# Border of a graph layer and the next hop: two subtractions moved behind VectorE's last additions, and a product's accumulators paired otherwise

## The chip, the cores and the metric

The kernel runs on one core of one Trainium2 chip. Times are microseconds of device time for one execution; lower is better. Several executions give a median; one more execution, on the same kernel, was recorded by the hardware profiler, and all views of the profile come from that one.

## What is computed

Two graph layers on features `x` of 8 batches, 2048 nodes and 64 channels, with one row-normalised adjacency matrix `adj` of 2048 x 2048. Each layer ends in a residual and a layernorm. Cut to what matters:

```python
# layer 0: I, A, 2AA-I applied to x, then a 64x64 weight of each node's own (16 parts), bias
w = einsum('nd,dkio->nkio', embedding, weight)          # d = 16, k = 3
x_g = einsum('knm,bmc->bnkc', A_stack, x)
x = layernorm(x + einsum('bnki,nkio->bno', x_g, w) + b)
# layer 1: x, Ax, 2AAx-x (twice, with the same A), one shared weight
x = layernorm(x + x_cat @ weight + bias)
```

Every row of `adj` holds one value at its nonzero places, so the kernel splits it into a 0/1 pattern and a factor per row, and multiplies with the pattern. The features go into the matmuls as two parts, a high half (rounded to fp32r) and a low half (the rest), one matmul for each.

## The kernel before

The program has five stretches: two hops (products of the pattern with the features) for layer 0; the node mixing of layer 0, node tile by node tile (16 tiles of 128 nodes); a third hop and a fourth for layer 1; and the final layernorm. The change lies at the border between the mixing of the last tile (t = 15) and the third hop.

**Order.** Each engine carries out its instructions in the order in which the program writes them (`ordered`), so the order is written out by hand. In the mixing loop, `at[n]` lists the side work that is written ahead of piece n of a tile, and `at[8]` what is written after the last piece.

**Mixing of a tile** (`mix0`, L402). Eight pieces, each a product in PSUM (L409), which is then weighted and added up. Pieces of four channels' worth (`by_four`, L425) are added into `acc` by VectorE, four instructions each (L433). Pieces by batch go over ScalarE into `aside` (L423), which GpSimd sums (L440, three instructions) and adds to `acc` (L445). For the last tile the pieces are (0,0), (0,1), (0,4), (1,0), (0,5), (1,1), (1,4), (1,5); the last two are VectorE's. Then comes the projection of the tile before (`project`, L458: matmuls L466, six ScalarE copies L475), and the layernorm of this tile (L362 to L380), whose result is transposed on TensorE (L300) inside the third hop, at the steps (0,5) and (0,6) of it (`last_transposed`, `last_projected`).

**The third hop** (`seven_products`, L586, called at L833). A product of 2 x 2 blocks in seven products, each with 8 contraction steps, 56 steps in all. Each step has 8 matmuls (L664): for each of two halves of the output (i), first the high half and then the low half of the features, each over two column blocks. A product accumulates in two PSUM buffers, `sums[p % 2]`, one for i = 0 and one for i = 1, so products alternate between two pairs of buffers. The high halves are made by ScalarE (`high`, L234), the low halves by VectorE (`low`, L238: features minus high half), the pattern operand by a ScalarE cast (L652). For the first four steps these are written early (`early`, L842), within the last tile's mixing:

```python
            at[6] += [(("add",), 0), lambda: got.update(hT=transpose(h, "hT")), lambda: early(2, "y_high")]
            at[7] += [(("sum",), 1), lambda: early(2, "y_low"), lambda: early(3, "y_high")]
            at[8] += [(("add",), 1), lambda: early(3, "y_low")]
```

**PSUM.** One pool of four buffers, two banks each (`bank`, L84), serves all of it: pieces, transposes, projections and the hop's sums. A new tile takes a buffer when it is first written, and its first matmul waits for the last reader of what was there. The four sums of the hop are named at the first step (L659):

```python
                if p == 0 and kk == 0:
                    sums.extend([bank("accT") for _ in range(2)] for _ in range(2))
                acc, hl, S = sums[p % 2], got["hl"], got["s"]
```

Of the kernel before, what the change touches and what calls it, by code (L numbers as in the profile page):

```python
# [39 lines left out]
def pattern(  # L40
# [43 lines left out]
    def bank(name):  # L84

        return psum.tile([P, 2, 512], F32, tag="ps", name=name)
# [146 lines left out]
    def high(src, to):  # L233
        ordered(nc.scalar.copy(to[0], src))  # L234
# [348 lines left out]
        (S4, "B22", (0, 1)), ((0, 1), "B21", (0, 0)), ((1, 1), "T4", (1, 0)),  # L583
    )

    def seven_products(s, to, sums, more, wait=4, raw=()):  # L586

        kept = {}

        def sum_of_y(kk, name):


            def quarter(half, b):
                return z[s][kk + KK * (half - 1)][:, (b - 1) * BC : b * BC]

            def add(to, a, b, op):
                ordered(nc.vector.tensor_tensor(to, a, b, op))  # L600
                return to

            if name[0] == "B":
                return quarter(int(name[1]), int(name[2]))
            if name == "T2":
                if kk % 2 == 0:
                    tag = "acc" if kk < KK // 2 else "ln_sq"
                    kept[kk // 2] = work.tile([P, 2, BC], F32, tag=tag, name="t2")
                y = kept[kk // 2][:, kk % 2]
                return add(y, add(y, quarter(2, 2), quarter(1, 2), ALU.subtract), quarter(1, 1), ALU.add)  # L610
            if name == "T4":
                y = kept[kk // 2][:, kk % 2]
                return add(y, y, quarter(2, 1), ALU.subtract)
            y = xcpool.tile([P, BC], F32, tag="ln_xc", name="y")
            a, b = (quarter(1, 2), quarter(1, 1)) if name == "T1" else (quarter(2, 2), quarter(1, 2))
            return add(y, a, b, ALU.subtract)

        def step(p, kk):
            which, name, finished = PRODUCTS[p]

            def sum_y(got):
                got["y"] = sum_of_y(kk, name)

            def y_high(got):
                hl = hpool.tile([P, 2, BC], F32R, tag="hl", name="hl")
                got["hl"] = [hl[:, 0], hl[:, 1]]
                if name == "T4":
                    got["y"] = kept[kk // 2][:, kk % 2]
                elif name[0] == "B":
                    sum_y(got)  # L630
                high(got["y"], got["hl"])

            def y_low(got):
                low(got["y"], got["hl"])

            def load_sum(got):
                if which in raw:
                    return
                got["raw"] = rawp.tile([P, 2, Q], BF16, tag="raw", name="raw")
                if which == (0, 0):  # L640
                    load(nc.sync, got["raw"], corner[kk])
                elif isinstance(which, tuple):
                    load(nc.sync, got["raw"], quarters[kk, :, which[0]])
                else:
                    load(nc.sync, got["raw"], sums_of[kk, :, :, which, :].rearrange("g m n -> m g n"))

            def operands(got):
                if which in raw:
                    got["s"] = places(slab(kk, 0, HALF))
                else:  # L650
                    s = spool.tile([P, 2, Q], F32R, tag="s", name="s")
                    ordered(nc.scalar.copy(s, got["raw"]))  # L652
                    got["s"] = s.rearrange("p g n -> p (g n)")
                if loads:
                    load(nc.sync, *loads.pop(0))

            def use(got):
                if p == 0 and kk == 0:
                    sums.extend([bank("accT") for _ in range(2)] for _ in range(2))  # L659
                acc, hl, S = sums[p % 2], got["hl"], got["s"]  # L660
                for i in range(2):
                    for h in range(2):
                        for c in range(2):
                            nc.tensor.matmul(  # L664
                                acc[i][:, c], lhsT=hl[h][:, i * P : (i + 1) * P], rhs=S[:, c * 512 : (c + 1) * 512],
                                start=(kk == 0 and h == 0), stop=(kk == KK - 1 and h == 1),
                            )
                if p == 3:
                    sum_of_y(kk, "T4")
                for f in more.get((p, kk), ()):  # L670
                    f()
                if kk < KK - 1:
                    return
                if p < 6:
                    todo.extend([nothing] * wait)
                for i in range(2):
                    for c in range(2):
                        todo.append(lambda i=i, c=c: put(acc[i][:, c], i, c))
                while p == 6 and todo:
                    todo.pop(0)()  # L680
                todo.extend(more.get(p, ()))

            def put(src, i, c):

                src = src.rearrange("p (t n) -> p t n", n=P)

                def add(where, first, op=ALU.add):
                    ordered(nc.vector.tensor_tensor(to(*where, i, c), to(*first, i, c), src, op))  # L688

                product = PRODUCTS[p]  # L690
                if product is M1:
                    ordered(nc.scalar.copy(to(0, 0, i, c), src))
                elif product is M6:
                    add((0, 1), (0, 0))
                elif product is M7:
                    add((1, 0), (0, 1))
                elif product is M5:
                    add((1, 1), (1, 0))
                    add((0, 1), (0, 1))
                else:  # L700
                    add(finished, finished, ALU.subtract if product is M4 else ALU.add)

            before = [(5, sum_y)] if name in ("T1", "T2", "T3") else []
            return before + [(4, y_high), (3, y_low), (4, load_sum), (3 if which in raw else 2, operands), (0, use)]

        return [step(p, kk) for p in range(7) for kk in range(KK)]
# [116 lines left out]
    def quarter_back(a, b, which):  # L823
# [11 lines left out]
        (0, 6): [last_projected],  # L835
        **{(2 + t // KK, t % KK): [lambda t=t: add_bias(t)] for t in range(NT)},
        3: quarter_back(1, 1, 1), 4: quarter_back(0, 1, 0), 5: quarter_back(0, 0, 1),
    }, wait=2)

    third_got = {}  # L840

# [11 lines left out]
    s = ("load_sum", "operands")  # L853
# [3 lines left out]
    for t in range(NT):  # L857
        got, last = {}, t == NT - 1
        at = [[] for _ in range(9)]
        n1, n2, n3 = [lambda: next(norm)] * 3 if t else [nothing] * 3  # L860

        if not last:
            following, of_x, of_hop, of_second = coming
            of_hop = of_hop()
            at[1] += [go(of_x)] * (1 if t else 3)
            at[2] += [go(of_hop), n1, go(of_hop), go(of_hop), n2]
            if t + 2 < NT:
                at[2] += [lambda: times_r(t + 2)]
                at[4] += [lambda: got.update(coming=operands(t + 2))]
            at[3] += [n3, go(of_second), lambda: got.update(acc=begin_sum(t + 1))]  # L870
            at[4] += [go(of_second), go(of_second)]
            at[6] += [(("sum", "add"), 0)]
            at[7] += [lambda: got.update(hT=transpose(h, "hT"))] if t else []
            pieces = [(0, 0), (0, 4), (0, 5), (1, 2), (0, 1), (1, 3), (1, 4), (1, 5)]
        else:
            at[1] += [n1, n2]
            at[2] += [n3, lambda: early(0, "y_high", *s)]
            at[3] += [(("sum",), 0), lambda: early(0, "y_low")]
            at[4] += [lambda: early(1, "y_high", *s)]
            at[5] += [lambda: early(1, "y_low")]  # L880
            at[6] += [(("add",), 0), lambda: got.update(hT=transpose(h, "hT")), lambda: early(2, "y_high")]
            at[7] += [(("sum",), 1), lambda: early(2, "y_low"), lambda: early(3, "y_high")]
            at[8] += [(("add",), 1), lambda: early(3, "y_low")]
            pieces = [(0, 0), (0, 1), (0, 4), (1, 0), (0, 5), (1, 1), (1, 4), (1, 5)]
        norm_now = mix0(t, tt, acc, at, pieces)
        if t:
            project(t - 1, got["hT"])
        if "coming" in got:
            coming = got["coming"]
            next(coming[1])  # L890
            next(coming[1])
        norm = norm_now
        h = next(norm)
        if not last:
            tt, acc = following, got["acc"]
# [34 lines left out]
    sums = keep.tile([P, G, B], F32, tag="sums", name="sums")  # L930
# [445 lines left out]
```

## Time and profile before

| what | value |
|---|---|
| median of three executions | 764.98 us (764.36 to 765.15) |
| the profiled execution | 764.04 us, of which the span is 762.3 us |
| TensorE matmuls, busy | 753.6 us, 99% of the span |
| VectorE, busy | 560.2 us, 73% |
| ScalarE, busy | 406.7 us, 53% |
| GpSimd, busy | 269.7 us, 35% |
| granted TensorE clock | 0.999 |
| third hop's and second hop's matmuls (L664) | 896, 390 ns each |

How to read it: the engines work side by side, so an engine's busy time says little unless it sets the end. The end of a matmul is modelled and overlaps with the next, so a recorded gap on TensorE is shorter than the time lost; starts are the surer measure. In a row of the timeline the first number is the start in us from the span's start, the second how long the row lasts, `x4` how many instructions are merged in it, and the brackets say how long the engine was idle ahead of it and for whom. In the list of waits, the numbers are the total, how often, and the longest.

### The profile page before, as it was taken

How to read it: one execution, taken by the hardware profiler on the slowest of the kernel's cores; microseconds unless marked ns; L12 is line 12 of the kernel's file. 1: busy time of each engine (PE TensorE's matmuls, PEld its weight loads, DVE VectorE, ACT ScalarE, POOL GpSimd, SP SyncE). 2: the span in 40 equal slices, each digit the busy share in tenths (PEclk: the TensorE clock that was granted, in tenths of full speed). 3: DMA queues.
4: the chain of work that ended last, by engine and by line, in shares of the span. 5: the costliest groups of instructions: out<-in, count | busy, mean ns of one | idle time of the engine just before them, and what ended most of it. 6: DMA issues, size and time to landing. Idle time of an engine off the chain costs nothing.

```text
span 762.3 us, 16926 instructions
## 1 busy us (share of the span) xinstructions
PE 753.6 (99%) x6634; PEld 660.6 (87%) x6634; DVE 560.2 (73%) x1159; ACT 406.7 (53%) x896; POOL 269.7 (35%) x297
## 2 busy tenths in 40 slices
PE   9999999999999999999999999999999999999996
PEld 6888888888889999999999999998888888888885
DVE  6768867678757888888888888877688648668663
ACT  5456533877745555555555555558887663112111
POOL 0000000000026877777777777777100000011441
PEclk9999999999999999999999999999999999999999
DMA  8998996555520000000000000003454444565631
GB/s 325 346 393 282 350 312 233 154 177 162 171 69 17 20 20 15 20 18 16 16 16 17 15 16 3 2 16 87 135 167 151 130 154 142 175 177 175 208 127 46
DMA packets 73558, 96.69 MB, mean 127 GB/s; under 512 B 4864, under 2 KB 48384, under 8 KB 73344
## 3 DMA queue, kind: packets, MB, share of 16 engines
q1 hardware_dynamic: 62064, 76.66, 31.8%
q10 hardware_dynamic: 11408, 18.89, 6.6%
q8 instruction: 54, 0.88, 0.5%
q14 instruction: 32, 0.26, 0.1%
HBM read 76.65 MB, written 18.87 MB: 125 GB/s over the span
## 4 chain that ended last, share of the span: by engine, by line
PE 98%; DVE 1%; issue 0%; ACT 0%; DVEq 0%
PE pm L409 36%; PE accT L664 27%; PE acc L254 15%; PE a L254 10%; PE accT L254 6%; PE pu L466 2%; PE pt L300 1%; PE first L143 1%; PE accT L814 1%; DVE acc L433 1%; PE accT L466 0%; PE accT L153 0%; PE accT L300 0%; ACT sq L994 0%; DVE z L289 0%
## 5 line engine op out<-in xcount | busy, mean ns | idle before, releaser
L433 DVE SCALAR_TENSOR_TENSOR acc<-pm,pack_sb,acc 128x256 f32<-128x256 f32 x376 | 181.0, 482 | 44.0 <-PE pm L409 32.0
L409 PE MATMUL pm<-wh,hl 64*128 64x512 f32 (+1 forms) x1332 | 208.0, 303 | 0.0
L664 PE MATMUL accT<-s,hl 128*128 128x512 f32 x896 | 205.9, 390 | 0.8 <-DVE acc L433 0.8
L409 PE MATMUL pm<-wm,parts 64*128 64x512 f32 (+1 forms) x1332 | 203.5, 296 | 0.0
L409 PE MATMUL pm<-wl,parts 64*128 64x512 f32 (+1 forms) x1332 | 203.4, 296 | 0.0
L664 PEld LDWEIGHTS accT<-s,hl 128*128 128x128 f32 x896 | 167.5, 188 | 36.5 <-issue 1.6
L409 PEld LDWEIGHTS pm<-wh,hl 64*128 64x128 f32 x1332 | 130.9, 187 | 4.0 <-issue 0.4
L409 PEld LDWEIGHTS pm<-wl,parts 64*128 64x128 f32 x1332 | 130.8, 187 | 3.7
L409 PEld LDWEIGHTS pm<-wm,parts 64*128 64x128 f32 x1332 | 130.5, 187 | 3.8
L652 ACT CAST s<-raw 128x1024 fp32r<-128x1024 bf16 x104 | 109.9, 1057 | 37.9 <-ACT hl L234 23.4
L254 PE MATMUL acc<-hl,s 128*128 128x512 f32 x512 | 116.8, 390 | 0.0
L254 PEld LDWEIGHTS acc<-hl,s 128*128 128x128 f32 x512 | 96.2, 188 | 20.5 <-issue 0.3
L423 ACT ACTIVATE aside<-pm,pack_sb 128x128 f32<-128x128 f32 x272 | 74.0, 383 | 48.9 <-PE pm L409 48.1
L715 POOL TENSOR_TENSOR z<-z,rrow 128x512 f32<-128x512 f32 x16 | 21.1, 1320 | 212.4 <-DVE z L688 212.4
L234 ACT CAST hl<-z 128x256 fp32r<-128x256 f32 (+1 forms) x96 | 47.7, 515 | 60.1 <-PE acc L254 24.1
L440 POOL TENSOR_TENSOR aside<-aside 128x1024 f32<-128x1024 f32 (+2 forms) x51 | 75.3, 1476 | 4.2 <-ACT aside L423 1.6
L254 PE MATMUL a<-hl,s 128*128 128x512 f32 (+1 forms) x352 | 73.4, 370 | 0.0
L254 PEld LDWEIGHTS a<-hl,s 128*128 128x128 f32 x352 | 61.9, 188 | 11.3
L320 POOL TENSOR_TENSOR parts<-parts 128x512 fp32r<-128x512 f32 x45 | 58.2, 1294 | 35.1 <-DVE parts L314 27.5
L238 DVE TENSOR_TENSOR hl<-z,hl 128x512 fp32r<-128x512 f32 (+1 forms) x96 | 54.7, 577 | 12.9 <-ACT hl L234 10.1
L287 POOL TENSOR_TENSOR z<-z,got 128x512 f32<-128x512 f32 x3 | 4.8, 1631 | 144.4 <-ACT got L286 144.4
L254 PE MATMUL accT<-hl,s 128*128 128x512 f32 x192 | 44.3, 390 | 0.0
(136 smaller groups left out, 814.4 us busy)
## 6 DMA issues: line engine op xcount, KB each, us to landing
raw<-in_adj SPq DMA_DIRECT2D x58, 512.0 KB, 6.1
raw<-sums_of SPq DMA_DIRECT2D x64, 256.0 KB, 2.9
sums_of<-z ACTq DMA_DIRECT2D x16, 512.0 KB, 6.6
raw<-quarters SPq DMA_DIRECT2D x32, 256.0 KB, 2.7
raw<-in_adj SPq DMA_DIRECT2D x16, 384.0 KB, 3.5
quarters<-seen ACTq DMA_DIRECT2D x16, 256.0 KB, 5.8
xt<-in_xT SPq DMA_DIRECT2D x16, 256.0 KB, 2.7
z<-in_x SPq DMA_DIRECT2D x15, 256.0 KB, 6.8
```

Of the source, the lines that this page charges most:

```text
L234: ordered(nc.scalar.copy(to[0], src))
L238: ordered(nc.vector.tensor_tensor(to[1], src, to[0], ALU.subtract))
L254: nc.tensor.matmul(accs[i], lhsT=s[:, i * P : (i + 1) * P], rhs=hl[h], start=(first and h == 0), stop=(last and h == 1),)
L320: ordered(nc.gpsimd.tensor_tensor(mixed, mixed, low, ALU.add))
L409: nc.tensor.matmul(pm[:, j], lhsT=tt[k][n][q, lhsT, :], rhs=w_parts[n][k][q, ds, :], start=(k == 0 and n == 0), stop=(k == 2 and n == 2),)
L423: ordered(nc.scalar.activation(aside[g][d // DG][:, d % DG, :, i, :], pm[:, :, d, :], AF.Copy, scale=e(d)))
L433: ordered(nc.vector.scalar_tensor_tensor(part, got, e(dg * DG + d), part, ALU.mult, ALU.add))
L440: ordered(nc.gpsimd.tensor_tensor(to, to, more, ALU.add))
L466: nc.tensor.matmul(pm[:, j, i * 3 * C : (i + 1) * 3 * C], lhsT=hT[q, 2 * g + i, :], rhs=v[q], start=True, stop=True,)
L652: ordered(nc.scalar.copy(s, got["raw"]))
L664: nc.tensor.matmul(acc[i][:, c], lhsT=hl[h][:, i * P : (i + 1) * P], rhs=S[:, c * 512 : (c + 1) * 512], start=(kk == 0 and h == 0), stop=( ...
L715: ordered(nc.gpsimd.tensor_tensor(to, to, r, ALU.mult))
```

## The change

Two edits. In the mixing of the last tile, the low half of the hop's step 2 is written after the last piece instead of ahead of it, next to the low half of step 3, which was there before. And the third hop pairs its four PSUM buffers by a new argument: the first product of the hop names the first and the third of them, the second product the second and the fourth, where before they were the first two and the last two. The second hop, which calls the same function, keeps the old pairs by default.

```diff
-    def seven_products(s, to, sums, more, wait=4, raw=()):
+    def seven_products(s, to, sums, more, wait=4, raw=(), pairs=((0, 1), (2, 3))):
...
                 if p == 0 and kk == 0:
-                    sums.extend([bank("accT") for _ in range(2)] for _ in range(2))
+                    four = [bank("accT") for _ in range(4)]
+                    sums.extend([four[a], four[b]] for a, b in pairs)
...
         3: quarter_back(1, 1, 1), 4: quarter_back(0, 1, 0), 5: quarter_back(0, 0, 1),
-    }, wait=2)
+    }, wait=2, pairs=((0, 2), (1, 3)))
...
-            at[7] += [(("sum",), 1), lambda: early(2, "y_low"), lambda: early(3, "y_high")]
-            at[8] += [(("add",), 1), lambda: early(3, "y_low")]
+            at[7] += [(("sum",), 1), lambda: early(3, "y_high")]
+            at[8] += [(("add",), 1), lambda: early(2, "y_low"), lambda: early(3, "y_low")]
```

## The prediction

> **What bounds the kernel now.** I read four views in this order: the page's busy table, the list of what TensorE waited for, the chain of waits cut to the border between layer 0 and the third hop, and the timelines of the engines in that stretch.
>
> ```profile
> PE 753.6 (99%) x6634; PEld 660.6 (87%) x6634; DVE 560.2 (73%) x1159; ACT 406.7 (53%) x896; POOL 269.7 (35%) x297
> PE 98%; DVE 1%; issue 0%; ACT 0%; DVEq 0%
> ```
>
> ```profile
> PE first L143 <- DVE part L144: 1.3, 1, 1.3
> PE accT L664 <- DVE acc L433: 0.8, 1, 0.8
> ```
>
> TensorE is busy for 99% of the span and is 98% of the chain that ends last. Its waits on other engines come to two in the whole run: 1.3 us at the start, and 0.8 us at the first matmuls of the third hop (L664), for VectorE's L433. The change lies at the second. Nothing else on TensorE can be won there, so the question is how much of one short stall goes, and whether it stays gone.
>
> The chain of waits around it (start, us, what), and the timelines of TensorE, VectorE and GpSimd:
>
> ```profile
> 525.90 0.48 DVE acc L433
> 526.38 0.06 DVE hl L238
> 526.45 1.02 issue
> 527.47 0.48 DVE acc L433
> ...
> 529.01 0.50 DVE acc L433
> 529.51 0.14 issue
> 529.65 10.24 PE accT L664 x44
> ```
>
> ```profile
> 526.16 0.29 PE L409 MATMUL pm<-wm,parts 64*128 64x256 f32 x2
> 526.28 1.47 PE L466 MATMUL pu<-v,hT 64*128 64x192 f32 x16
> 527.69 1.20 PE L664 MATMUL accT<-s,hl 128*128 128x512 f32 x4
> 529.65 2.53 PE L664 MATMUL accT<-s,hl 128*128 128x512 f32 x10 [0.76 <-DVE acc L433]
> ```
>
> ```profile
> 524.34 2.04 DVE L433 SCALAR_TENSOR_TENSOR acc<-pm,pack_sb,acc 128x256 f32<-128x256 f32 x4 [1.63 <-PE pm L409]
> 526.30 1.24 DVE L238 TENSOR_TENSOR hl<-z,hl 128x256 fp32r<-128x256 f32 x1
> 527.47 2.03 DVE L433 SCALAR_TENSOR_TENSOR acc<-pm,pack_sb,acc 128x256 f32<-128x256 f32 x4
> 529.42 0.42 DVE L238 TENSOR_TENSOR hl<-z,hl 128x256 fp32r<-128x256 f32 x1
> ```
>
> ```profile
> 524.87 4.63 POOL L440 TENSOR_TENSOR aside<-aside 128x1024 f32<-128x1024 f32 x3 [1.57 <-ACT aside L423]
> 529.64 0.79 POOL L445 TENSOR_TENSOR acc<-acc,aside 128x256 f32<-128x256 f32 x1
> ```
>
> What is to be seen: the last piece's product on TensorE ends at 526.16 + 0.29 = 526.45. VectorE could add it then, having finished the piece before at 524.34 + 2.04 = 526.38. It has the low half of the hop's step 2 in front, which takes 1.24 us because it meets GpSimd's sum; the same form takes 0.42 us at 529.42. So the four additions start at 527.47 and end at 527.47 + 2.03 = 529.50, and 0.15 us later TensorE goes on. Meanwhile it had done four matmuls of step 0 (527.69) and stood.
>
> **How large the stall really is.** The row says 0.76 us, but matmul ends are modelled and overlap. By starts: the 44 matmuls from 529.65 take 10.24 us, so (10.24 - 0.39)/43 = 0.23 us from start to start (0.39 is one matmul's length in the page). The first four begin at 527.69 and last 1.20, so the fourth began at 527.69 + 1.20 - 0.40 = 528.49 and the fifth was due at 528.72. It came at 529.65, and its successor (instruction by instruction in the timeline) 0.31 instead of 0.23 later. The loss is 0.93 + 0.08 = 1.0 us. That is the most that this border can return.
>
> **What the Trainium skill says.** "Perfetto Trace Analysis", section "Identifying the Most-Contended Engine", says that matmul busy time is a poor measure of headroom since pipelined matmuls look smaller. The trace agrees in kind: 0.76 us of recorded idle stands for 1.0 us of lost starts. "GPSIMD Engine Reference", section "Specifications", says that GpSimd shares its SBUF interfaces with VectorE and contends with VectorE instructions that have two SBUF inputs. The trace agrees: the low half (both tensors in SBUF) takes 1.24 us beside L440 and 0.42 us at 529.42 after it, while L433, with one operand in PSUM, takes 0.48 each beside the same L440. "PSUM — Partial Sum Buffer", section "Terms", says that two engines on one bank at once are an error; so a product that reuses a bank has to wait for the last reader, which is the wait at 529.65.
>
> **The change, part by part.**
>
> 1. *The low half of step 2 goes behind the last piece.* No instruction is added or removed. In VectorE's order the four L433 of piece (1,5) now follow the four of piece (1,4). They start when both the product (526.45) and VectorE (526.38) are ready. For piece (1,4) the handover from product to L433 was 0.05 us (its last pair starts at 524.00, ends at 524.29, L433 starts at 524.34), so I take 526.45 + 0.05 = 526.50. That is 527.47 - 526.50 = 0.97 us earlier. They last 2.04 us as before: the first four ran beside the same GpSimd sum and took 2.04. They end at 528.54, TensorE is let go at 528.54 + 0.15 = 528.69, against 528.72 when it is due. So the stall goes nearly whole: between 0.93 (if the restart still pays its 0.08 and a little more) and 1.0. I take the plain shift, 0.97 us.
>
> 2. *What now waits behind.* Low half 2 starts at 528.54 while GpSimd is in L440. Alone it costs 0.42, beside GpSimd up to 1.27 (the longest such instruction in this stretch): it ends between 528.96 and 529.81. Low half 3 follows, ending between 529.4 and 531.1; before it ended at 529.84. Step 2's high matmuls begin after 16 matmuls, at 527.69 + 16 x 0.23 + 0.1 = 531.5, its low ones two matmuls later at 531.9: at least 2.1 us of room. Step 3 starts at 533.3: at least 2.2 us of room. TensorE gets one more wait, on low half 2 at step 2's third matmul; before, the wait for L433 covered it. Behind it stands the rest of TensorE, but it is met long before. Cost: zero.
>
> 3. *LayerNorm of the last tile.* Behind the low halves on VectorE stands the reduction L362, which waits for GpSimd's L445 (530.43). L445 needs L440, which ends at 529.50 whatever the additions do. If low half 2 makes L440 slower, as the earlier low half may have made its second part, it is by 0.1 us or so. From L362 the chain goes to GpSimd's L380, which ends at 536.78 + 1.22 = 538.00, and TensorE transposes its result at 539.81. With the border 0.97 earlier that is 538.84, so 0.84 us of room remain. Bounds: nothing lost, up to 0.9 lost in case B below.
>
> 4. *The hop's first product in other banks.* The call gives the pairs (0,2) and (1,3) of the four buffers. By the names, the second half of the first product would then take the buffer of the projection (L466), which ScalarE empties by its first three L475 copies: 527.16 + 1.75/2 = 528.04, ahead of 528.49. But a buffer is handed out at its first use, not where it is named. In the instruction lists of the two programs the second buffer that the hop writes is in both the one that piece (1,5) had, banks 0 and 1; the names alone have changed places, and TensorE still waits there for VectorE. The last tile's transpose goes to banks 6 and 7 in both. TensorE, ScalarE, GpSimd and the DMA queues keep their orders. So this part costs and brings nothing: 0, with bounds 0 and 0.03 (the rest of the stall).
>
> Sum: -0.97 us. The profiled execution took 764.04 us (span 762.30 and 1.74 around it), so it becomes 763.07. The median shown is 764.98, 0.94 above the profiled one, and I apply the same difference to it: **764.0 us**.
>
> **Does it stay gone?** All later work of TensorE has no recorded wait, so it moves forward whole if its suppliers keep up. ScalarE's operand casts (L652) are the closest: read one by one, the smallest distance from a cast's end to its step's first matmul is 1.08 us, in the thirteenth step at 552.99. ScalarE reaches that stretch after waiting itself for TensorE (1.05 us at L475, 543.21; 2.25 us at L306, 540.32), so it moves along. The end of the run is TensorE's too.
>
> **The rivals.**
>
> A. *The stall goes, nothing takes its place:* 764.0, as above. If the second part did give other banks, the result would be 764.98 - 1.00 = 763.98, which a time can't tell from it. Chance 0.80.
>
> B. *The gain is eaten by the layernorm chain.* If both low halves meet GpSimd (two times 1.27 - 0.42 = 0.85, so 1.7 us in all) and hold L362 and L445 back by that, TensorE would wait 1.7 - 0.84 = 0.86 at the transpose: 764.9. For it: low halves do meet GpSimd at 526.30. Against it: one collision was already there before, and has only changed its place. Chance 0.10.
>
> C. *Slower.* The same chain, at the same place (the transpose at 539.81), turns the sign once it is late by more than 0.84 + 0.97 = 1.81 us. Three collisions of 0.85 more than before make it 2.55 - 1.81 = 0.74 us slower, 765.7; four make it 1.59 us slower, 766.6. For it: several low halves and L600 additions of VectorE lie between the border and L380. Against it: from 530 to 560 GpSimd works 4.2 us of 30, so there is little to meet. Chance 0.05, of which 0.03 for four.
>
> D. *More than the stall.* Nothing in the trace lets the border give more than 1.0 us; it would need a loss that no row shows. 763.2 or less. Chance 0.05.
>
> **How the numbers follow.** A measurement of this kernel can tell about 0.2%, which is 1.53 us: below 763.45 counts as faster, above 766.5 as slower. A's forecast lies inside, 0.55 us above the lower bound. The three runs spread over 0.79 us, so I leave 0.10 of A's 0.80 to fall below. Faster 0.15 (0.10 + D's 0.05), slower 0.03 (C with four collisions), same 0.82, the rest. The range takes A's 763.98 less one spread, 763.2, up to B with nothing left, 765.0.
>
> **What would show it.** In the profile after: no TensorE wait on L433 at the hop's start, or one under 0.1 us; L433's last four starting within 0.1 us of the product's end and directly behind the four before; both low halves after them, one of them over 0.6 us; the transpose of the last tile without a wait. Wrong would be: L433 still late, so that something other than the low half held it; a new wait at L300 (B or C); or a border won and a longer rest.

## The result, and the profile after

The changed kernel takes 762.85 us, the median of 18 executions (762.47 to 763.86), against 764.50 us for the kernel before in 18 executions beside it (763.63 to 765.20). The ratio is 0.9979, with a 95% interval of 0.9972 to 0.9986: 1.65 us less, and between 1.1 and 2.1. The sign and the place were right; the forecast of 764.0, and its range down to 763.2, were too high. The profiled execution took 762.75 us with a span of 760.9, where the one of before took 764.04 with 762.3.

The busy row of the page and all of TensorE's waits in the changed kernel:

```profile
PE 752.6 (99%) x6634; PEld 660.0 (87%) x6634; DVE 560.0 (74%) x1159; ACT 407.2 (54%) x896; POOL 270.0 (35%) x297
```

```profile
PE first L143 <- DVE part L144: 1.3, 1, 1.3
```

The wait on L433 is gone; one row is left of two. The timelines of VectorE, TensorE and GpSimd at the border, in the changed kernel (its matmuls of the hop are L665, since the file is one line longer):

```profile
523.60 4.21 DVE L433 SCALAR_TENSOR_TENSOR acc<-pm,pack_sb,acc 128x256 f32<-128x256 f32 x8 [1.64 <-PE pm L409]
527.73 1.44 DVE L238 TENSOR_TENSOR hl<-z,hl 128x256 fp32r<-128x256 f32 x2
529.81 0.69 DVE L362 TENSOR_REDUCE s<-acc 128x8 f32<-128x512 f32 x1 [0.64 <-POOL acc L445]
```

```profile
525.43 0.29 PE L409 MATMUL pm<-wm,parts 64*128 64x256 f32 x2
525.55 1.47 PE L466 MATMUL pu<-v,hT 64*128 64x192 f32 x16
526.95 3.31 PE L665 MATMUL accT<-s,hl 128*128 128x512 f32 x13
```

```profile
524.26 4.63 POOL L440 TENSOR_TENSOR aside<-aside 128x1024 f32<-128x1024 f32 x3 [1.70 <-ACT aside L423]
```

The eight additions of the last two pieces stand in one row, the two low halves behind them, and TensorE's matmuls run on without a break. Against the profile before, and counted from the last product's start (526.17 there, 525.44 here), the hop's ninth matmul comes 0.96 us earlier. That is the 0.97 us of the forecast. From there to the start of the last matmul both take 224.68 us. The rest of the difference between the two spans lies elsewhere: 0.69 us in TensorE's first matmuls at 5 to 8 us, where the program is the same, less 0.31 us after the last matmul (6.96 us in place of 6.65). So the two profiles agree with the forecast, and the 18 executions do not. What was open was why the executions gained 1.65 us.

### The profile page after: what moved, and what is told of

The parts are those of the page before. It is cut to its first block, busy times and chain, and to the rows that moved or that the text cites. A ratio compares the mean times of both kernels' runs of the same rounds, so it can differ in the third digit from the quotient of the medians.

```text
span 760.9 us, 16926 instructions
## 1 busy us (share of the span) xinstructions
PE 752.6 (99%) x6634; PEld 660.0 (87%) x6634; DVE 560.0 (74%) x1159; ACT 407.2 (54%) x896; POOL 270.0 (35%) x297
## 4 chain that ended last, share of the span: by engine, by line
PE 99%; DVE 0%; ACT 0%; issue 0%; DVEq 0%
PE pm L409 36%; PE accT L665 27%; PE acc L254 15%; PE a L254 10%; PE accT L254 6%; PE pu L466 3%; PE pt L300 1%; PE accT L815 1%; PE first L143 1%; PE accT L466 0%; PE accT L153 0%; PE accT L300 0%; ACT sq L995 0%; DVE z L289 0%; DVE got L1000 0%
## 5 line engine op out<-in xcount | busy, mean ns | idle before, releaser
L433 DVE SCALAR_TENSOR_TENSOR acc<-pm,pack_sb,acc 128x256 f32<-128x256 f32 x376 | 181.0, 482 | 43.9 <-PE pm L409 31.8
L665 PE MATMUL accT<-s,hl 128*128 128x512 f32 x896 | 205.8, 390 | 0.0
L665 PEld LDWEIGHTS accT<-s,hl 128*128 128x128 f32 x896 | 167.5, 188 | 35.6 <-issue 0.7
L652 ACT CAST s<-raw 128x1024 fp32r<-128x1024 bf16 x104 | 109.9, 1057 | 37.8 <-ACT hl L234 24.5
L423 ACT ACTIVATE aside<-pm,pack_sb 128x128 f32<-128x128 f32 x272 | 74.2, 384 | 48.8 <-PE pm L409 48.1
L440 POOL TENSOR_TENSOR aside<-aside 128x1024 f32<-128x1024 f32 (+2 forms) x51 | 75.4, 1478 | 4.4 <-ACT aside L423 1.7
```

What stands on the lines that cost most here:

```text
L423: ordered(nc.scalar.activation(aside[g][d // DG][:, d % DG, :, i, :], pm[:, :, d, :], AF.Copy, scale=e(d)))
L433: ordered(nc.vector.scalar_tensor_tensor(part, got, e(dg * DG + d), part, ALU.mult, ALU.add))
L440: ordered(nc.gpsimd.tensor_tensor(to, to, more, ALU.add))
L665: nc.tensor.matmul(acc[i][:, c], lhsT=hl[h][:, i * P : (i + 1) * P], rhs=S[:, c * 512 : (c + 1) * 512], start=(kk == 0 and h == 0), stop=( ...
```

## The experiments

In each case the time is compared with executions of the kernel before on the same chip. Two more runs, e7 and e8, are one profiled execution each of the kernel before.

| run | what it is | us | before, us | ratio (95% interval) |
|---|---|---|---|---|
| e1_pairs_alone | second edit alone | 764.24 | 764.44 | 0.9995 (0.9987 to 1.0003) |
| e2_low_alone | first edit alone | 762.71 | 764.44 | 0.9977 (0.9967 to 0.9986) |
| e3_both_in_front | two low halves in front | 767.03 | 764.44 | 1.0035 (1.0022 to 1.0049) |
| e4_low2_in_the_idle | low half one piece earlier | 763.22 | 764.44 | 0.9983 (0.9975 to 0.9992) |
| e5_cast_behind | ScalarE's cast of step 1 moved | 763.22 | 764.51 | 0.9983 (0.9975 to 0.9990) |
| e6_change_and_cast_behind | the change and e5 | 763.08 | 764.51 | 0.9980 (0.9972 to 0.9988) |
| e9_other_banks_in_fact | another bank in fact, low half in front | 762.88 | 764.51 | 0.9980 (0.9973 to 0.9987) |
| e10_sum_in_two | GpSimd's first sum in two, without a break | 764.40 | 764.51 | 0.9997 (0.9989 to 1.0005) |
| e11_sum_in_chain | GpSimd's first sum in two, with a break | 763.18 | 764.64 | 0.9981 (0.9974 to 0.9988) |

### The two edits one by one

The second edit alone (e1) is the change without its last hunk, and the first edit alone (e2) is that hunk on the kernel before.

> The second edit alone: the hop pairs its buffers as after, the low half of step 2 stays ahead of the last piece. Theory 1 (the banks stay what they were, and the whole change is the low half): 0.0 us against before, within 0.3 us, the profile shows the same stall of TensorE at L665's fifth matmul (0.76 us recorded). Theory 2 (the other banks free the first product from VectorE): the stall is gone and the time falls by about 1 us or more. Theory 3 (each of the two edits brings a part of the 1.65 us measured): 0.5 to 0.8 us faster.

> The first edit alone: the low half of step 2 behind the last piece, the old pairs. Theory 1: the same as the full change, and what is over 0.97 us in the measured 1.65 us is scatter of the executions, so 0.9 to 1.7 us faster than before with the stall gone from the profile. Theory 2: no gain, or under 0.3 us. Theory 3: about 0.97 us and not more.

e1 is no faster: 0.20 us, with an interval across zero. Its instructions, with their operands' addresses and their waits, are those of the kernel before without exception; e2's are those of the changed kernel. So the second edit does nothing in this program, and the first is all of it: 1.73 us. Since e1 is the same program as before, its profile is also a second one of the kernel before, and it differs from the first. ScalarE, GpSimd, VectorE and TensorE in e1:

```profile
521.97 1.05 ACT L652 CAST s<-raw 128x1024 fp32r<-128x1024 bf16 x1 [0.76 <-DMA raw<-corner]
```

```profile
525.16 3.80 POOL L440 TENSOR_TENSOR aside<-aside 128x1024 f32<-128x1024 f32 x2 [2.35 <-ACT aside L423]
```

```profile
525.90 1.92 DVE L238 TENSOR_TENSOR hl<-z,hl 128x256 fp32r<-128x256 f32 x1
527.74 2.03 DVE L433 SCALAR_TENSOR_TENSOR acc<-pm,pack_sb,acc 128x256 f32<-128x256 f32 x4
```

```profile
527.19 1.20 PE L665 MATMUL accT<-s,hl 128*128 128x512 f32 x4
529.92 1.37 PE L665 MATMUL accT<-s,hl 128*128 128x512 f32 x5 [1.53 <-DVE acc L433]
```

TensorE waits 1.53 us where it waited 0.76 us, because the low half takes 1.92 us in place of 1.24 and starts 0.10 us later after the last product. The chain that leads there reads from the top. ScalarE's pattern cast of the hop's step 1 waited 0.76 us for its DMA. Behind that cast, in ScalarE's order, stand the activations L423 of piece (1,1); GpSimd's first sum L440 needs them and starts later. VectorE's low half starts in time but does not end before that sum does. The same rows of the profile before have no such wait:

```profile
521.67 1.05 ACT L652 CAST s<-raw 128x1024 fp32r<-128x1024 bf16 x1
522.62 2.17 ACT L423 ACTIVATE aside<-pm,pack_sb 128x128 f32<-128x128 f32 x8
```

There the pattern landed at 521.65, while ScalarE's instruction ahead of the cast was still running (to 521.71), so no wait shows. This gave theory 4: the stall's size is set by a DMA four steps up the chain, and the profile before had caught an execution in which it landed early.

### The dose doubled, and another place

In e3 the low half of step 3 goes ahead of the last piece too:

```diff
-            at[7] += [(("sum",), 1), lambda: early(2, "y_low"), lambda: early(3, "y_high")]
-            at[8] += [(("add",), 1), lambda: early(3, "y_low")]
+            at[7] += [(("sum",), 1), lambda: early(2, "y_low"), lambda: early(3, "y_high"), lambda: early(3, "y_low")]
+            at[8] += [(("add",), 1)]
```

> The dose doubled: the low half of step 3 goes ahead of the last piece too, so that two low halves stand there. Theory 1: the last piece's additions start when the second low half ends. If it meets GpSimd's second sum they start at about 529.0 instead of 527.47, and the run is 1.5 us slower than before; without a meeting 0.45 us slower. TensorE's gap grows by the same. Rival (the border is covered by something else, for example the projection's copies on ScalarE): no difference, within 0.3 us.

It is 2.59 us slower, so the direction holds, and the size is more than the 1.5 us expected. VectorE and TensorE in e3:

```profile
525.65 3.29 DVE L238 TENSOR_TENSOR hl<-z,hl 128x256 fp32r<-128x256 f32 x2
528.86 2.03 DVE L433 SCALAR_TENSOR_TENSOR acc<-pm,pack_sb,acc 128x256 f32<-128x256 f32 x4
```

```profile
531.04 1.17 PE L664 MATMUL accT<-s,hl 128*128 128x512 f32 x4 [2.81 <-DVE acc L433]
```

Both low halves wait for a sum of GpSimd each, and TensorE waits 2.81 us, 1.28 more than in e1. Only five executions stand behind the time, from 765.71 to 768.21. The profile is of the fastest of them, which is 1.27 us slower than the median before, about as much as its stall is longer; what the others lose beyond that was not settled.

In e4 both halves of step 2 go one piece earlier, ahead of the additions of piece (1,4), where VectorE had been idle for 1.63 us:

```diff
-            at[5] += [lambda: early(1, "y_low")]
-            at[6] += [(("add",), 0), lambda: got.update(hT=transpose(h, "hT")), lambda: early(2, "y_high")]
-            at[7] += [(("sum",), 1), lambda: early(2, "y_low"), lambda: early(3, "y_high")]
+            at[5] += [lambda: early(1, "y_low"), lambda: early(2, "y_high")]
+            at[6] += [(("add",), 0), lambda: early(2, "y_low"), lambda: got.update(hT=transpose(h, "hT"))]
+            at[7] += [(("sum",), 1), lambda: early(3, "y_high")]
```

> Another place for the low half of step 2: with its high half one piece earlier, it goes ahead of the additions of piece (1,4), where VectorE sat idle for 1.63 us. Theory 1 (what counts is that nothing stands ahead of the last piece's additions): the stall goes as with the full change, 0.9 to 1.7 us faster than before, equal to e2 within 0.4 us. Rival (the early high half delays ScalarE's activations of piece (1,1) and with them GpSimd's sum or the transposed tile): equal to before or up to 0.5 us slower.

1.22 us faster, and the wait on L433 is gone from its profile too. It is 0.51 us behind e2, a little more than expected, with intervals that overlap; whether that is the high half's 0.3 us on ScalarE ahead of L423 is not known. In its trace the layernorm's last instruction on GpSimd (L380) ends at 538.14 and TensorE starts the transpose of its result at 538.22, so with a somewhat later DMA TensorE would wait there; no trace here shows that wait. e4 shows that "behind the last piece" is not what matters: as long as the hop waits for that piece's buffer, nothing that can be held up may stand ahead of its additions.

### The chain cut at ScalarE

Theory 4 says that the low half may stay in front, if GpSimd's sum is early enough. In e5 the kernel before keeps both low halves, and only the cast of step 1 goes behind the activations:

```diff
-            at[4] += [lambda: early(1, "y_high", *s)]
+            at[4] += [lambda: early(1, "y_high", "load_sum")]
...
-            at[6] += [(("add",), 0), lambda: got.update(hT=transpose(h, "hT")), lambda: early(2, "y_high")]
+            at[6] += [(("add",), 0), lambda: got.update(hT=transpose(h, "hT")), lambda: early(2, "y_high"), lambda: early(1, "operands")]
```

> The kernel before, both low halves where they were; only ScalarE's pattern cast of the hop's step 1 (L652), which waits for its DMA, goes behind the activations L423 of piece (1,1). Theory 4 (the size of the stall is set by when GpSimd's first L440 ends, since the low half can't pass it; L440 starts when ScalarE's L423 are done, and these stand behind the cast and its DMA): L440 starts about 1 us or more earlier, the low half ends within 0.6 us of the last product, the additions L433 start under 0.5 us late, TensorE's recorded wait is under 0.4 us or gone, and the run is 1.2 to 1.7 us faster than before, without touching the low half. Rival (the low half costs what it costs in front of the last piece, or the excess over 0.97 us comes from the start of the run): no more than 0.4 us faster, with the stall at 0.7 us or more.

> The full change and the cast of step 1 moved behind as in e5. Theory 4: the stall is gone already, so the same time as the full change, 762.5 to 763.2, within 0.4 us of e2; less scatter at most. Rival (the late DMA costs something of its own besides the stall): faster than e2 by 0.5 us or more.

e5 is 1.29 us faster. Its GpSimd, VectorE and TensorE:

```profile
523.53 4.64 POOL L440 TENSOR_TENSOR aside<-aside 128x1024 f32<-128x1024 f32 x3 [0.83 <-ACT aside L423]
```

```profile
525.70 0.53 DVE L238 TENSOR_TENSOR hl<-z,hl 128x256 fp32r<-128x256 f32 x1
526.15 2.03 DVE L433 SCALAR_TENSOR_TENSOR acc<-pm,pack_sb,acc 128x256 f32<-128x256 f32 x4
```

```profile
527.09 5.12 PE L664 MATMUL accT<-s,hl 128*128 128x512 f32 x20
```

The sum starts 2.04 us ahead of the last product's start (525.58), where it was 1.30 ahead in the profile before and 0.51 in e1. The low half, in the same place as before, takes 0.53 us, and TensorE does not stop long enough for a row. What is left of the stall by starts is 0.23 us (the hop's ninth matmul 3.75 us after the last product's start, against 3.52 in the changed kernel). The rival's 0.4 us is excluded by the interval. e6 is 1.43 us faster, the same as the full change within its interval: once the low half is behind, the early sum brings nothing more.

Two more profiles of the kernel before were to show how much the stall changes from one execution to the next:

> The kernel before, one more look. Theory 4: TensorE's recorded wait at the fifth matmul of the hop is 0.76 us plus what ScalarE waits for the DMA of step 1's pattern at L652, within 0.15 us, whatever these are in this execution. Rival: the wait is 0.7 to 0.8 us whatever ScalarE's wait, or moves without it.

> The kernel before once more, the same expectation as the look ahead of it: recorded wait of TensorE = 0.76 us + ScalarE's wait for the DMA at L652 of step 1, within 0.15 us. The two looks and the two at hand show how much the stall changes between executions of one program.

ScalarE's cast and TensorE's wait in e7:

```profile
521.92 1.05 ACT L652 CAST s<-raw 128x1024 fp32r<-128x1024 bf16 x1 [0.65 <-DMA raw<-corner]
```

```profile
529.87 1.37 PE L664 MATMUL accT<-s,hl 128*128 128x512 f32 x5 [1.42 <-DVE acc L433]
```

All four profiles of one program, with the loss in starts taken as the hop's ninth matmul's distance from the last product's start, less the 3.52 us that it has without a stall:

| profile | ScalarE waits for the DMA | TensorE's recorded wait | 0.76 + ScalarE's wait | loss in starts |
|---|---|---|---|---|
| the profile before | 0.00 us | 0.76 us | 0.76 us | 0.96 us |
| e1 | 0.76 us | 1.53 us | 1.52 us | 1.71 us |
| e7 | 0.65 us | 1.42 us | 1.41 us | 1.60 us |
| e8 | 0.56 us | 1.33 us | 1.32 us | 1.53 us |

The rule held to 0.01 us. Three profiles of four lose 1.5 to 1.7 us, which is what the executions gained, and their executions took 764.45 to 764.57 us, near the median of 764.5. The profile before, at 764.04, is the odd one. The other traces say the same of the DMA: from its issue to its landing the load of step 1's pattern took 3.2 to 3.3 us in three of the thirteen (before, after and e11) and 3.7 to 4.1 us in the other ten. Nor does the rest of the run come into it: from the hop's ninth matmul to the start of the last matmul all thirteen take 224.67 to 224.70 us.

### The bank in fact

The second edit changes names only. In e9 it is made to do what its words say, with the low half left in front. A buffer is handed out at first use, so a one-element write by VectorE takes the last piece's buffer for another of the four sums:

```diff
                 for i in range(2):
+                    if p == 0 and kk == 0 and i == 1 and pairs[0] == (0, 2):
+                        ordered(nc.vector.memset(four[1][0:1, 0, 0:1], 0.0))
```

> The second edit made to do what its words say, with the low half of step 2 left ahead of the last piece: a one-element memset on VectorE takes the buffer of piece (1,5) in the name of the second product's sum, so that the second half of the hop's first product gets the projection's buffer, which ScalarE empties. Theory (the wait at the fifth matmul is only for the bank, and low halves 2 and 3 are not needed before steps 2 and 3): the recorded wait is gone though L433 of the last piece stays as late as before, and the run is 1.2 to 1.7 us faster than before. If the layernorm of the last tile, which follows the late L433, is then late for its transpose, some of it comes back as a wait at L300: 0.5 to 1.2 us faster. Rival (low halves or something else on VectorE hold TensorE anyhow): no gain.

VectorE and TensorE in e9 (its L667 is the hop's matmul):

```profile
525.61 1.83 DVE L238 TENSOR_TENSOR hl<-z,hl 128x256 fp32r<-128x256 f32 x1
527.36 2.03 DVE L433 SCALAR_TENSOR_TENSOR acc<-pm,pack_sb,acc 128x256 f32<-128x256 f32 x4
```

```profile
526.99 5.28 PE L667 MATMUL accT<-s,hl 128*128 128x512 f32 x22
```

The low half waits as long as ever and the additions are as late as ever, but TensorE does not care: 1.63 us faster. So either edit would have been enough alone, had both done what they say, and the wait at the fifth matmul was for the bank alone.

### What holds the low half

Theory 4 has one more link: that the low half can't pass GpSimd's sum. e10 splits that sum of 1024 elements in two:

```diff
-            for to, more in ((one, other), (one[:, :2], one[:, 2:]), (one[:, 0], one[:, 1])):
+            first = [(one[:, :2], other[:, :2]), (one[:, 2:], other[:, 2:])] if t == NT - 1 and g == 1 else [(one, other)]
+            for to, more in (*first, (one[:, :2], one[:, 2:]), (one[:, 0], one[:, 1])):
```

e11 differs from it in that the second part adds to what the first has written, and so waits for it:

```diff
-            first = [(one[:, :2], other[:, :2]), (one[:, 2:], other[:, 2:])] if t == NT - 1 and g == 1 else [(one, other)]
+            first = [(one[:, :2], other[:, :2]), (one[:, :2], other[:, 2:])] if t == NT - 1 and g == 1 else [(one, other)]
```

> The kernel before, with the first sum L440 of the last tile's second group (1024 elements a partition, 2.38 us) written as two of 512. Theory 4b (VectorE's low half can't run beside a GpSimd instruction that is under way, it ends about 0.28 us after that instruction): the low half ends 0.28 us after the first short sum, about 1.1 us earlier; the additions start that much earlier and the run is 0.8 to 1.3 us faster than before. Rival (they merely share: the low half is slowed in proportion while GpSimd works at all): the low half takes about as long as before, under 0.3 us of gain.

> The kernel before, the first L440 in two of 512 elements again, but now the second one adds into what the first one wrote, so that it has to wait for the first and GpSimd stands for the 0.08 us between two of its instructions that every such pair shows in the traces. The order of the additions changes with it. In e10 the two ran into each other without such a break and VectorE's low half ended 0.29 us after the second. Theory 4c (the low half gets in only where GpSimd stops between two instructions): it ends about 0.3 us after the first short sum, about 1.1 us earlier than in e10, the additions start that much earlier, and the run is 0.7 to 1.2 us faster than before. Rival (it waits for a fixed amount of GpSimd's work or time): no gain, as in e10.

e10 missed its expectation: no gain. GpSimd's two short sums and VectorE's low half in e10 (its L441 is the sum):

```profile
525.00 1.29 POOL L441 TENSOR_TENSOR aside<-aside 128x512 f32<-128x512 f32 x1 [1.94 <-ACT aside L423]
526.26 1.26 POOL L441 TENSOR_TENSOR aside<-aside 128x512 f32<-128x512 f32 x1
```

```profile
526.25 1.55 DVE L238 TENSOR_TENSOR hl<-z,hl 128x256 fp32r<-128x256 f32 x1
```

The sums ran from 525.00 to 526.29 and from 526.26 to 527.52, with no break between them. The low half ended at 527.81, 0.29 us after the second short sum and not after the first. But it started only at 526.25, since the high half that it subtracts was ready no earlier (ScalarE made it from 525.75 to 526.22, behind the activations that the sums wait for). By then the first sum had 0.04 us left, and the second began within 0.01 us. So e10 was not the test that it was meant to be: an instruction that is held by the second sum alone would have ended at the same time.

In e11 the second sum waits for the first, and GpSimd stands still for 0.08 us between them:

```profile
525.65 1.01 DVE L238 TENSOR_TENSOR hl<-z,hl 128x256 fp32r<-128x256 f32 x1
526.58 2.03 DVE L433 SCALAR_TENSOR_TENSOR acc<-pm,pack_sb,acc 128x256 f32<-128x256 f32 x4
```

The low half ended at 526.66, 0.28 us after the end of the second short sum (526.38). The profile of e11 happens to have an early DMA, so the low half met the second short sum there too. The run is 1.46 us faster than before and e10 0.11. In both, the first short sum starts about 0.5 us earlier than the long one did, since it needs fewer of the activations, so the step from e10 to e11, about 1.35 us, goes with the break. That the low half gets in behind the first sum in an execution with a late DMA is read from the times only: had it met the second there as well, the loss would be about e10's (1.45 us in starts), and there would be no gain. Whether the break itself lets it in, or the second sum's later start, by which the low half comes first, is open. That the low half ends with a GpSimd instruction does not rest on these two runs: every low half between 520 and 533 us that took over 0.5 us, 43 in the thirteen traces, ended 0.28 to 0.29 us after the end of one.

## Why the prediction was wrong in its size

- *The stall as the mechanism, part 1, was right.* Between the two profiles the hop moved forward by 0.96 us of the 0.97 forecast. The additions followed the product at 525.76, 0.33 us after the last product's start, as the step said, and nothing took the stall's place. That the profiles agree says little of the size, since the forecast was read from the same profile of before. e2 shows that this edit is the whole change.
- *The step that failed is "how large the stall really is".* It took one execution's 1.0 us and said: "That is the most that this border can return." The low half's 1.24 us was read as a price. It was a distance to the end of GpSimd's sum, and that end hung on a DMA that ScalarE waits for in eight of the eleven traces that leave the cast in its place, for 0.53 to 0.86 us, and not in this one. e7 and e8 lose 1.60 and 1.53 us where the profile before lost 0.96. The term of the sum was 0.97 and should have been about 1.6. Case D, more than the stall, was held to need "a loss that no row shows"; the rows at hand did show all of its links (L440 waiting for L423, L423 behind L652, L652 fed by the load of `raw<-corner`), only not late; and the load had landed only 0.02 us before the cast began (521.65 and 521.67), so it had next to no room.
- *The starting point was 0.48 us off as well.* The forecast started from the median of three executions, 764.98; 18 of them have 764.50. Of the 1.15 us between 764.0 and 762.85, 0.48 is that, and 0.67 the stall's size. Either alone would have left the time inside the range: 764.98 - 1.65 = 763.33, and 764.50 - 0.97 = 763.53.
- *Part 2, room behind the change, was right:* the two low halves took 1.44 us together and delayed no matmul. *Part 3, the layernorm, was right:* L380 ended at 537.35, and TensorE came to the transpose at 538.12, with 0.77 us of room for the 0.84 forecast. B and C did not happen. But that room, too, was read from profiles with an early DMA: in e2, the same program as the changed kernel but in an execution with a wait of 0.53 us at the cast, L380 ended at 538.88 and the transpose began at 539.20, so 0.32 us were left. B was nearer than the two profiles say.
- *Part 4, the banks, was right.* e1 is the same program as the kernel before. That its words would be worth 1.00 us if true was too little, for the same reason as above: e9 gained 1.63.
- *What the Trainium skill could have given.* "SBUF — State Buffer", section "Who interferes with whom", says that VectorE's instruction with two SBUF inputs and a GpSimd instruction that reads SBUF lock each other out for the whole instruction. The traces agree: in nine of them the low half ahead of the last piece ended 0.28 to 0.29 us after a GpSimd sum. Read so, the 1.24 us is a wait with a variable end, and its upper bound, by an estimate from the traces, is GpSimd's 2.4 us and those 0.28 us, not 1.27.

## What to carry to other kernels

A stall in a profile is one draw. Before its length becomes the gain of removing it, follow it up engine by engine until it ends in something that is fixed, or in a DMA; if it ends in a DMA with little room, the length in the trace may be the lucky one, and a second profile of the same program costs little. An instruction that is slow only beside another engine may, like this low half, have no price of its own: its end was tied to the other's. And a bank that a program names is not the bank it gets when buffers are handed out at first use.

## What was not expected of the hardware

- VectorE's low half (two SBUF inputs) took 0.42 us alone and 0.53 to 1.92 us beside GpSimd's sums, and it ended 0.28 to 0.29 us after the end of one however long it had waited. Splitting a sum of 2.4 us into two of 1.29 and 1.26 us that followed each other without a break (e10) gained nothing; with 0.08 us between them (e11) the run was 1.46 us faster. That a sum which follows without a break holds the low half like the sum before it is not shown, since in e10 the two met for 0.04 us only. L433, with one input in PSUM, took 0.47 to 0.49 us beside the same sums throughout.
- The load of step 1's pattern (256 KB) landed 3.2 to 3.3 us after its issue in three traces and 3.7 to 4.1 us in ten, in e1, e7, e8 and the profile before in one and the same program (3.2 us there, 3.8 to 4.0 in the others). Why is open.
- In e3, with TensorE standing for 3 us, the five executions' mean granted clock lay between 0.999 (765.71 us) and 0.993 (768.21 us), not quite in the order of the times (768.01 us had 0.997); in every other execution here it was 0.997 to 0.999. Whether the longer stall lowers the clock was not tried.
